# A graph layer's first stage in pairs of node columns, its node update in runs of consecutive nodes, its flag in the loop, its last groups in batches of their own

## The chip, the cores and the metric

The kernel runs on one core of one Trainium2 chip. The metric is the device time of one execution in microseconds (us), the median of several runs. A core has TensorE (PE, with its weight loads shown apart as PEld), VectorE (DVE), ScalarE (ACT), GpSimd (POOL) and SyncE (SP), each with an instruction queue of its own, and 16 DMA engines.

## What is computed

One layer of a graph network on 12,500 nodes of 64 features and 412,500 edges of 32 features, the edges sorted by receiver (`dst`):

```python
h = jnp.maximum(_layernorm(x, axis=-1), 0.0)
msg_in = jnp.concatenate([h[src], h[dst], edge_attr_32], axis=-1)
messages = act(msg_in @ W1 + b1) @ W2 + b2
att_logits = act(msg_in @ Wa1 + ba1) @ Wa2 + ba2
att = jax.nn.softmax(att_logits, axis=0)
aggregated = jax.ops.segment_sum(messages * att, dst, num_segments=12500)
upd_in = jnp.concatenate([h, aggregated], axis=-1)
return x + (act(upd_in @ Wu1 + bu1) @ Wu2 + bu2)
```

`act` is swish, and the softmax runs over all edges. Everything is float32.

## The kernel before

Nodes lie as `(p b)`: partition p holds NB = 98 consecutive nodes, and a "node column" b is one node of each of the 128 partitions. Edges lie in NG = 403 groups of K = 8 blocks of 128.

**First stage** (L168 to L243). Seven chunks of CB = 14 node columns are loaded (`xc`, L175), normalised on VectorE and ScalarE (L204 to L218), and transposed on TensorE, four columns to a PSUM tile `pt` (L224). VectorE copies that to `hT` (L225), whose row 64 is a one for the bias, set by GpSimd (L184). One matmul for each column (L228) multiplies it with the sender half of `w_node`; ScalarE copies the result to `ts` (L230), and SyncE writes it to the table `ts_d` (L231); `hT` goes to `hT_d` chunk by chunk (L232). In the third chunk `windows` (L186) makes each edge's place in its group's window (`dloc`) and a number for the flag. Then the same matmuls with the receiver half give `tr` and the table `tr_d` (L233 to L243).

**Loop over groups** (`one_pass`, L513). `load` (L351), two groups ahead, gathers 8 blocks of sender rows out of `ts_d` with 8 indirect DMAs issued by GpSimd (L358) into one of 8 buffers `gs`, loads a window of `tr_d` and the edge features through SyncE, and multiplies them on TensorE (L385) with a selection matrix made on VectorE (L381). `begin` (L390) adds both and starts tanh on ScalarE; swish is taken as x(1 + tanh x) on halved weights. `end` (L393) makes the message (L399), then the attention logits (L402 to L407). Four groups make a batch; `top` (L411) takes a batch's maximum through a transposition on TensorE, and `weigh` (L425) its weights. `sum_up` (L488), about five groups behind, does for one group after another `out_of` (L455, ScalarE), `put` (L465, VectorE, adds to `sums` and notes the maximum used), `project` (L460, TensorE) and `by_node` (L440: eight weight matrices on VectorE, then the matmuls of L452). `batch`, `starts` and `size` say which groups share a batch: fours, then groups 400 and 401, then group 402. From the third last group on, L534 to L539 do the sums left over. `pin` keeps these instructions in the order of the program. PSUM tiles named `mt` share one buffer. From group 16 on, `node_bias` (L252) and `node_rest` (L267) prepare for every four node columns the parts of the update that do not depend on the edges.

**Node update** (L553 to L596). Thirteen steps of eight node columns (the last of two). `fac` (L576, ScalarE) is the exponential that brings a node's sum to the last maximum. Two products on VectorE (L581) of `sums`, one over the total, and `fac` give `uT`, four columns on each half of the partitions; `bu` is added (L584), tanh on ScalarE (L586), a product (L587), a matmul for each pair of columns (L591), `x` added (L593), result out (L596). `sums` is stored by node, so node column b is every 98th element.

**Flag** (L599 to L608). The largest entry of `far` decides whether the general method must run afterwards. Three tiles named `res` stand between, so that their buffers' writes are waited for; `wrong` is loaded by all engines (L246) and a branch follows (L248).

Of the kernel before, what the change touches and what calls it, by code (L numbers as in the profile page):

```python
# [43 lines left out]
ALU = mybir.AluOpType  # L45
# [29 lines left out]
def gnn_kernel(ctx: ExitStack, tc: tile.TileContext, n_edges, x, src, dst, dst_row, first, edge,  # L75
# [14 lines left out]
    hT_d = dram.tile([D, NB, P], F32, name="hT_d")  # L90
    bu_d = dram.tile([U, NB, P], F32, name="bu_d")
    xb_d = dram.tile([NP, D], F32, name="xb_d")
# [5 lines left out]
    w_node = const.tile([D + 1, 2 * C + U], F32, name="w_node")  # L98
    nc.vector.memset(w_node[D:D + 1, C:2 * C], 0.0)
    nc.sync.dma_start(w_node[:D, 0:U], Wa1[0:D, :])  # L100
    nc.sync.dma_start(w_node[:D, U:C], W1[0:D, :])
    nc.sync.dma_start(w_node[D:D + 1, 0:U], ba1[None, :])
    nc.sync.dma_start(w_node[D:D + 1, U:C], b1[None, :])
    nc.scalar.dma_start(w_node[:D, C:C + U], Wa1[D:2 * D, :])
    nc.scalar.dma_start(w_node[:D, C + U:2 * C], W1[D:2 * D, :])
    nc.scalar.dma_start(w_node[:D, 2 * C:], Wu1[0:D, :])
    nc.scalar.dma_start(w_node[D:D + 1, 2 * C:], bu1[None, :])

    nc.vector.tensor_scalar(w_node[:, 0:2 * C], w_node[:, 0:2 * C], 0.5, None, op0=ALU.mult)
# [16 lines left out]

    wa2 = across(Wa2, U, "wa2")
# [40 lines left out]
    with tc.tile_pool(name="node1", bufs=1) as node1, \  # L168
# [14 lines left out]
        hT = node1.tile([D + 1, NB, P], F32, name="hT")  # L183
        nc.gpsimd.memset(hT[D:D + 1], 1.0)  # L184
# [14 lines left out]

        for c in range(0, NB, CB):  # L200
            if c == min(2 * CB, NB - CB):
                windows()
# [17 lines left out]
            for b in range(0, CB, 4):  # L220
                n = min(4, CB - b)
                pt = node_ps.tile([D, 4, P], F32, name="pt")
                for i in range(n):
                    nc.tensor.transpose(pt[:, i, :], h[:, b + i, :], ident)  # L224
                nc.vector.tensor_copy(hT[:D, c + b:c + b + n, :], pt[:, :n, :])  # L225
                pn = node_ps.tile([P, 4, C], F32, name="pn")
                for i in range(n):
                    nc.tensor.matmul(pn[:, i, :], hT[:, c + b + i, :], w_node[:, 0:C],  # L228
                                     start=True, stop=True)
                nc.scalar.copy(ts[:, b:b + n, :], pn[:, :n, :])  # L230
            nc.sync.dma_start(ts_d.rearrange("(p b) f -> p b f", b=NB)[:, c:c + CB, :], ts)  # L231
            nc.scalar.dma_start(hT_d[:, c:c + CB, :], hT[:D, c:c + CB, :])  # L232
        for c in range(0, NB, CB):  # L233
            tr = node.tile([P, CB, C], F32, name="tr")
            for b in range(0, CB, 4):
                n = min(4, CB - b)
                pn = node_ps.tile([P, 4, C], F32, name="pn")
                for i in range(n):
                    tc.keep_in_program_order(
                        nc.tensor.matmul(pn[:, i, :], hT[:, c + b + i, :], w_node[:, C:2 * C],  # L240
                                         start=True, stop=True))
                nc.vector.tensor_copy(tr[:, b:b + n, :], pn[:, :n, :])  # L242
            nc.scalar.dma_start(tr_d[:NP, :].rearrange("(p b) f -> p b f", b=NB)[:, c:c + CB, :], tr)  # L243
# [8 lines left out]
def node_bias(tc, b, v, work, ps):  # L252

    nc = tc.nc
    NB, w_node = v["NB"], v["w_node"]
# [3 lines left out]
    nc.sync.dma_start(hb[:D, :n, :], v["hT_d"][:, b:b + n, :])  # L259
    pb = ps.tile([P, 4, P], F32, name="mt")  # L260
    nc.tensor.matmul(pb[:U, :n, :], w_node[:, 2 * C:], hb[:, :n, :], start=True, stop=True)
    bu = work.tile([U, 4, P], F32, name="bu")
    nc.scalar.copy(bu[:, :n, :], pb[:U, :n, :])
    nc.sync.dma_start(v["bu_d"][:, b:b + n, :], bu[:, :n, :])
# [13 lines left out]
def one_pass(tc, n_edges, v):  # L278
# [5 lines left out]
    ts_d, tr_d, bu_d, edge, dst_row = (v[k] for k in ("ts_d", "tr_d", "bu_d", "edge", "dst_row"))  # L284
# [4 lines left out]
    starts = list(range(0, NG - 1, B)) + [NG - 1]  # L289
# [5 lines left out]
    with ExitStack() as ctx:  # L295
# [27 lines left out]
        with tc.tile_pool(name="work2", bufs=2) as work2, \  # L323
# [69 lines left out]
            def end(g):  # L393

                s = batch[g]
                if g == starts[s]:
                    lgs[s] = small.tile([P, B * K], F32, name="lg")
                gs, th = gss.pop(g), pes.pop(g)
                pin(nc.vector.scalar_tensor_tensor(acts[g % ACTS][:, :, 0:U], th[:, :, U:C], 1.0,  # L399
                                                   gs[:, :, U:C], op0=ALU.add, op1=ALU.mult))  # L400
# [7 lines left out]
                if g == starts[s] + size[s] - 1:  # L408
                    mts[s] = top(s)

# [102 lines left out]
            for g in range(NG):  # L513
                more = None
                if done <= g - B - 1 and g < NG - 1 or g == NG - 2 and done < starts[batch[g]]:
                    more, done = sum_up(done), done + 1
                begin(g)
                if more:
                    next(more)
# [14 lines left out]
                if g >= NG - 3:  # L534
                    upto = starts[batch[g]] - 1 if g == NG - 3 else g + 1
                    for i in list(range(done, upto)) + [None, None] * (g > NG - 3):
                        for _ in sum_up(i):
                            pass
                    done = max(done, upto)  # L539
# [4 lines left out]
                if g == min(40, NG):  # L544
                    pin(nc.vector.tensor_reduce(far[:, 1:2], dloc, AX.X, ALU.min, negate=True))
                if g >= 16 and g // 4 - 4 < -(-NB // 4):
                    if g % 4 == 2:
                        node_bias(tc, (g // 4 - 4) * 4, v, work2, one_ps)
# [4 lines left out]
        with tc.tile_pool(name="upd1", bufs=1) as upd1, \  # L553
# [4 lines left out]
            sv = sums[:, :NP].rearrange("f (p b) -> f b p", b=NB)  # L558
# [3 lines left out]
            all_ps = upd_ps.tile([P, P], F32, name="worst_ps", bufs=1)  # L562
# [4 lines left out]
            assert NB % 2 == 0  # L567
            for c in range(0, NB, 2 * H):
                n = min(H, (NB - c) // 2)
                bu = work.tile([P, H, P], F32, name="bu_in")  # L570
                for h in range(2):
                    nc.sync.dma_start(bu[h * U:(h + 1) * U, :n, :], bu_d[:, c + h * n:c + (h + 1) * n, :])
                xb = work.tile([P, 2 * H, D], F32, name="xb")
                nc.sync.dma_start(xb[:, :2 * n, :], xb_v[:, c:c + 2 * n, :])
                fac = work.tile([U, 2 * H, P], F32, name="fac", bufs=2)
                nc.scalar.activation(fac[:, :2 * n, :], sv[U:, c:c + 2 * n, :], AF.Exp, bias=last[U:],  # L576
                                     scale=-1.0)
                uT = work.tile([P, H, P], F32, name="uT")
                for h in range(2):
                    cols = slice(h * n, (h + 1) * n)  # L580
                    nc.vector.scalar_tensor_tensor(  # L581
                        uT[h * U:(h + 1) * U, :n, :], sv[:U, c + h * n:c + (h + 1) * n, :], inv[:U],
                        fac[:, cols, :], op0=ALU.mult, op1=ALU.mult)
                nc.vector.tensor_tensor(uT[:, :n, :], uT[:, :n, :], bu[:, :n, :], ALU.add)  # L584
                th = work.tile([P, H, P], F32, name="th", bufs=2)
                nc.scalar.activation(th[:, :n, :], uT[:, :n, :], AF.Tanh, scale=0.5)  # L586
                nc.vector.scalar_tensor_tensor(uT[:, :n, :], th[:, :n, :], 1.0, uT[:, :n, :],  # L587
                                               op0=ALU.add, op1=ALU.mult)
                po = upd_ps.tile([P, H, 2, D], F32, name="po")
                for i in range(n):  # L590
                    nc.tensor.matmul(po[:, i, :, :], uT[:, i, :], wu2h, start=True, stop=True)  # L591
# [7 lines left out]
            worst = upd1.tile([P, 1], F32, name="worst")  # L599
            nc.vector.tensor_reduce(worst, far, AX.X, ALU.max)  # L600
# [226 lines left out]
```

## Time and profile before

| what | us |
|---|---|
| median of 3 runs | 4208.31 (4206.68 to 4211.77) |
| the profiled execution | 4211.1, its span 4209.4 |
| GpSimd busy | 3059.3 (73%) |
| VectorE busy | 2907.0 (69%) |
| TensorE matmuls busy | 2308.4 (55%) |
| ScalarE busy | 595.9 (14%) |
| DMA | mean 93 GB/s |

A line of groups reads: line, engine, operation, output and inputs, count, then busy time in us and the mean of one in ns, then the idle time of the engine before them and what ended most of it. A line of the timeline or of the chain of waits begins with start and duration in us. A line of waits reads: engine, tile and line, what it waited for, total us, times, longest. A matmul in float32 leaves two records.

### The profile page before, as it was taken

The page shows a single profiled execution, that of the slowest core. Times are in us where ns is not written, and L with a number is a line of the kernel's source. Part 1 is how long each engine was busy: PE and PEld are TensorE (multiplying, and loading weights), DVE is VectorE, ACT ScalarE, POOL GpSimd, SP SyncE. Part 2 cuts the span into 40 slices and gives each one's busy share as a digit, 9 for nine tenths or more (in the row PEclk, how much of TensorE's full clock was granted, in tenths as well). Part 3 has the DMA queues.
Part 4 walks back from the last instruction along what each step waited for, and adds up shares of the span by engine and source line. Part 5 has one row for each costly group of instructions (what it writes and reads, how often), then busy time and mean ns, then how long its engine had stood idle before and what let it go on. Part 6 is the DMA issues. An engine that isn't in the chain of part 4 may idle for free.

```text
span 4209.4 us, 44290 instructions
## 1 busy us (share of the span) xinstructions
PE 2308.4 (55%) x11224; PEld 1739.7 (41%) x11224; DVE 2907.0 (69%) x7735; ACT 595.9 (14%) x1212; POOL 3059.3 (73%) x3237
## 2 busy tenths in 40 slices
PE   7645554554555555555555555555554555555554
PEld 6434433443334443444434434444443444344443
DVE  6666766766767766766667667667676666676667
ACT  2211111111111111111111111111111111111113
POOL 2777777777777777777777777777777777777771
PEclk8666676666666656656566556655566565556665
DMA  5533333333333333233333332333333333323323
GB/s 192 147 91 101 95 103 102 94 103 101 95 94 91 81 90 89 80 90 83 86 89 82 88 89 80 89 87 82 90 82 88 89 80 90 89 80 89 84 71 101
DMA packets 227026, 392.13 MB, mean 93 GB/s; under 512 B 98889, under 2 KB 151178, under 8 KB 213706
## 3 DMA queue, kind: packets, MB, share of 16 engines
q0 software_dynamic: 103168, 211.49, 18.8%
q1 hardware_dynamic: 120580, 167.79, 15.0%
q10 hardware_dynamic: 3014, 9.92, 0.8%
q8 instruction: 93, 1.52, 0.2%
q14 instruction: 171, 1.40, 0.1%
HBM read 363.16 MB, written 25.72 MB: 92 GB/s over the span
## 4 chain that ended last, share of the span: by engine, by line
POOL 43%; issue 22%; DMA 18%; DVE 12%; PE 5%; DVEq 0%; ACT 0%; POOLq 0%; SPq 0%; ACTq 0%
POOL gs L358 43%; DMA gs<-ts_d,src_sb 18%; PE pe L385 2%; DVE gs L390 2%; DVE eo L381 2%; DVE wt L446 1%; PE sp L452 1%; DVE pe L402 1%; DVE lg L407 1%; DVE pe L404 1%; PE pn L228 1%; DVE sums L477 1%; DVE uT L581 0%; DVE acts L399 0%; PE mt L463 0%
## 5 line engine op out<-in xcount | busy, mean ns | idle before, releaser
L358 POOL DMA_INDIRECT gs<-ts_d,src_sb x3224 | 3047.3, 945 | 1058.0 <-issue 884.7
L385 PE MATMUL pe<-wins,eo 128*128 128x256 f32 x3224 | 1410.9, 614 | 1137.8 <-issue 1096.1
L385 PEld LDWEIGHTS pe<-wins,eo 128*128 128x128 f32 x3224 | 960.3, 312 | 1417.0 <-issue 1144.0
L390 DVE TENSOR_TENSOR gs<-pe,gs 128x1024 f32<-128x1024 f32 x403 | 491.9, 1221 | 1112.1 <-DMA gs<-ts_d,src_sb 1103.6
L391 ACT ACTIVATE pe<-gs 128x1024 f32<-128x1024 f32 x403 | 413.3, 1026 | 2782.2 <-DVE gs L390 2347.1
L446 DVE TENSOR_SCALAR wt<-iota_w,dloc,p 128x40 f32<-128x40 f32 x3224 | 724.6, 316 | 0.1
L452 PE MATMUL sp<-wt,acts 128*65 128x40 f32 x6448 | 599.7, 264 | 2.6 <-DVE wt L446 2.6
L452 PEld LDWEIGHTS sp<-wt,acts 128*65 128x65 f32 x6448 | 548.4, 176 | 29.1 <-DVE wt L446 3.1
L422 PE MATMUL mt<-ident,mx 128*128 128x128 f32 x102 | 48.5, 475 | 524.8 <-DVE sums L476 513.5
L404 DVE TENSOR_TENSOR pe<-pe,wa 128x512 f32<-128x512 f32 x403 | 281.6, 699 | 12.8
L402 DVE SCALAR_TENSOR_TENSOR pe<-pe,gs 128x512 f32<-128x512 f32 x403 | 280.6, 696 | 11.3
L399 DVE SCALAR_TENSOR_TENSOR acts<-pe,gs 128x512 f32<-128x512 f32 x403 | 271.8, 674 | 19.0 <-ACT pe L391 18.4
L407 DVE TENSOR_REDUCE lg<-pe 128x8 f32<-128x512 f32 x403 | 277.0, 687 | 10.4
L381 DVE TENSOR_SCALAR eo<-db,bj 64x256 f32<-64x256 int32 x806 | 269.9, 372 | 7.6
L463 PEld LDWEIGHTS mt<-ss,w2u 65*64 65x64 f32 x806 | 101.7, 179 | 384.8 <-issue 375.5
L422 PEld LDWEIGHTS mt<-ident,mx 128*128 128x128 f32 x102 | 18.6, 182 | 538.2 <-DVE sums L476 526.0
L463 PE MATMUL mt<-ss,w2u 65*64 65x40 f32 x806 | 153.1, 284 | 148.8 <-DVE gm L429 146.5
L433 ACT ACTIVATE scale<-fall 128x1 f32<-128x1 f32 x102 | 20.7, 203 | 511.2 <-DVE fall L432 511.2
L477 DVE COPY sums<-nmax 64x40 f32 x403 | 77.4, 192 | 8.7
L458 ACT COPY ss<-sp 65x40 f32<-65x40 f32 x403 | 73.4, 182 | 24.4 <-PE sp L452 24.1
L476 DVE TENSOR_TENSOR sums<-sums,mt 64x40 f32 x301 | 53.7, 178 | 5.4 <-PE mt L463 4.2
L240 PE MATMUL pn<-w_node,hT 65*128 65x128 f32 x196 | 41.7, 410 | 1.0 <-DVE tr L242 0.8
(96 smaller groups left out, 699.1 us busy)
## 6 DMA issues: line engine op xcount, KB each, us to landing
gs<-ts_d,src_sb POOLq DMA_INDIRECT x3224
eo<-in_edge_dram SPq DMA_DIRECT2D x100, 512.0 KB
db<-in_dst_row_dram SPq DMA_DIRECT2D x200, 256.0 KB
wins<-tr_d SPq DMA_DIRECT2D x806, 32.0 KB
ts_d<-ts SPq DMA_DIRECT2D x7, 896.0 KB
tr_d<-tr ACTq DMA_DIRECT2D x7, 896.0 KB
xc<-in_x_dram SPq DMA_DIRECT2D x7, 448.0 KB
hT_d<-hT ACTq DMA_DIRECT2D x7, 448.0 KB
```

The costliest lines, as they stand in the source:

```text
L358: nc.gpsimd.indirect_dma_start(out=gs[:, j, :], out_offset=None, in_=ts_d[:, :], in_offset=bass.IndirectOffsetOnAxis(ap=src_sb[:, t + j:t ...
L381: pin(nc.vector.tensor_scalar(eo[:WR, e], db[:, e], bj[:, g, h:h + 1], None, op0=ALU.is_equal))
L385: pin(nc.tensor.matmul(pe[:, 2 * q:2 * q + 2, :], eo[:, q * P:(q + 1) * P], win[:, q // 2, :, :], start=True, stop=True))
L390: pin(nc.vector.tensor_tensor(gss[g], pes[g], gss[g], ALU.add))
L391: pin(nc.scalar.activation(pes[g], gss[g], AF.Tanh))
L399: pin(nc.vector.scalar_tensor_tensor(acts[g % ACTS][:, :, 0:U], th[:, :, U:C], 1.0, gs[:, :, U:C], op0=ALU.add, op1=ALU.mult))
L402: pin(nc.vector.scalar_tensor_tensor(att, th[:, :, 0:U], 1.0, gs[:, :, 0:U], op0=ALU.add, op1=ALU.mult))
L404: pin(nc.vector.tensor_tensor(att, att, wa2[:, None, :].to_broadcast([P, K, U]), ALU.mult))
L407: pin(nc.vector.tensor_reduce(lgs[s][:, k:k + K], att, AX.X, ALU.add))
L446: pin(nc.vector.tensor_scalar(wt[:, j, :], iota_w[:, j // H, :], dloc[:, g * K + j:g * K + j + 1], p[:, k + j:k + j + 1], op0=ALU.is_equal ...
L452: pin(nc.tensor.matmul(sp, acts[g % ACTS][:, j, :], wt[:, j, :], start=j == 0, stop=j == K - 1))
L463: pin(nc.tensor.matmul(pp, w2u, sps.pop(g), start=True, stop=True))
```

## The change

- *First stage.* Two neighbouring node columns are transposed together (128 rows). `hT` holds pairs, without the row of ones. `w_pair` holds the weights twice on the diagonal, zeros elsewhere, so one matmul 256 wide serves two columns. ScalarE copies `hT`; PSUM tiles `pn` have three buffers. The sender table gets no bias; VectorE adds both biases in the copy of `tr`. `windows` comes behind the seven chunks, and `hT_d` is written in one transfer behind them. `node_bias` loads its part of `hT_d` in two transfers.
- *Node update.* The eight columns of a step are taken as runs of eight (or four) consecutive nodes: `fac`, `uT`, `bu` are stored node by node, column innermost. `node_bias` stores its result so in `bq_d`, and the matmul reads its weights `uv[:, :, i]` four elements apart.
- *Flag.* It is worked out at groups 44 and 45; at the end three memsets of one column take the `res` buffers.
- *Last groups.* Groups 400, 401 and 402 are batches of their own, and the sums left over are dealt to groups 399 to 402. In group 402 the message comes behind the logits, and `out_of` ahead of `begin`.

```diff
-    hT_d = dram.tile([D, NB, P], F32, name="hT_d")
+    hT_d = dram.tile([2 * D, NB // 2, P], F32, name="hT_d")
+    bq_d = dram.tile([U, NP], F32, name="bq_d")
...
+    w_pair = const.tile([P, 2, 2, C], F32, name="w_pair")
+    nc.vector.memset(w_pair, 0.0)
+    for r in range(2):
+        for h, eng in ((0, nc.sync), (1, nc.scalar)):
+            rows = slice(h * D, (h + 1) * D)
+            eng.dma_start(w_pair[rows, r, h, 0:U], Wa1[r * D:(r + 1) * D, :])
+            eng.dma_start(w_pair[rows, r, h, U:C], W1[r * D:(r + 1) * D, :])
...
-        nc.gpsimd.memset(hT[D:D + 1], 1.0)
...
+        nc.vector.tensor_scalar(w_pair, w_pair, 0.5, None, op0=ALU.mult)
         for c in range(0, NB, CB):
-            if c == min(2 * CB, NB - CB):
-                windows()
...
+            for b in range(0, CB, 8):
+                n = min(8, CB - b)
+                q = (c + b) // 2
+                pt = node_ps.tile([P, 4, P], F32, name="pt")
+                for i in range(n // 2):
+                    nc.tensor.transpose(pt[:, i, :], h[:, b + 2 * i:b + 2 * i + 2, :], ident)
+                nc.scalar.copy(hT[:, q:q + n // 2, :], pt[:, :n // 2, :])
+                for i in range(0, n, 4):
+                    m = min(4, n - i)
+                    pn = node_ps.tile([P, 4, C], F32, name="pn", bufs=3)
+                    for k in range(0, m, 2):
+                        nc.tensor.matmul(pn[:, k:k + 2, :], hT[:, q + (i + k) // 2, :], w_pair[:, 0],
+                                         start=True, stop=True)
+                    nc.scalar.copy(ts[:, b + i:b + i + m, :], pn[:, :m, :])
             nc.sync.dma_start(ts_d.rearrange("(p b) f -> p b f", b=NB)[:, c:c + CB, :], ts)
-            nc.scalar.dma_start(hT_d[:, c:c + CB, :], hT[:D, c:c + CB, :])
+        nc.scalar.dma_start(hT_d, hT)
+        nc.vector.tensor_scalar(bias, bias, 0.5, None, op0=ALU.mult)
+        windows()
...
-                nc.vector.tensor_copy(tr[:, b:b + n, :], pn[:, :n, :])
+                nc.vector.tensor_tensor(tr[:, b:b + n, :], pn[:, :n, :],
+                                        bias[:, None, :].to_broadcast([P, n, C]), ALU.add)
...
-    nc.sync.dma_start(hb[:D, :n, :], v["hT_d"][:, b:b + n, :])
+    for r in range(2):
+        nc.sync.dma_start(hb[:D, r:n:2, :], v["hT_d"][r * D:(r + 1) * D, b // 2:(b + n) // 2, :])
...
+    if quads and n == 4:
+        nc.scalar.copy(bu.rearrange("u b p -> u (b p)").rearrange("u (p b) -> u b p", b=4), pb[:U])
...
-    starts = list(range(0, NG - 1, B)) + [NG - 1]
+    starts = list(range(0, NG - 3, B)) + [NG - 3, NG - 2, NG - 1]
...
+                if g < NG - 1:
+                    message()
...
                     mts[s] = top(s)
+                if g == NG - 1:
+                    message()
...
-                if done <= g - B - 1 and g < NG - 1 or g == NG - 2 and done < starts[batch[g]]:
+                if done <= g - B - 1 or g >= NG - 3 and done < g:
                     more, done = sum_up(done), done + 1
+                if more and g == NG - 1:
+                    next(more)
                 begin(g)
...
-                if g >= NG - 3:
-                    upto = starts[batch[g]] - 1 if g == NG - 3 else g + 1
-                    for i in list(range(done, upto)) + [None, None] * (g > NG - 3):
+                if g >= NG - 4:
+                    upto = g + (-3, -1, 0, 1)[g - NG + 4]
+                    for i in list(range(done, upto)) + [None, None] * (g == NG - 1):
                         for _ in sum_up(i):
                             pass
+                        if i == done and g < NG - 1:
+                            weigh_upto(batch[g])
...
+                if g == min(44, NG):
+
+                    worst = small.tile([P, 1], F32, name="worst", bufs=1)
+                    pin(nc.vector.tensor_reduce(worst, far, AX.X, ALU.max))
+                    worst_ps = one_ps.tile([P, 4, P], F32, name="mt")[:, 0, :]
+                    pin(nc.tensor.transpose(worst_ps, worst.to_broadcast([P, P]), ident))
+                if g == min(45, NG):
+                    pin(nc.vector.tensor_reduce(worst, worst_ps, AX.X, ALU.max))
+                    pin(nc.vector.tensor_scalar(wrong, worst, 0.0, None, op0=ALU.is_gt))
...
-            sv = sums[:, :NP].rearrange("f (p b) -> f b p", b=NB)
+            sv = sums[:, :NP].rearrange("f (p b) -> f p b", b=NB)
...
+                    nc.sync.dma_start(bu[h * U:(h + 1) * U], bq_d[:, (c + h * n) * P:(c + (h + 1) * n) * P])
...
+                fac = work.tile([U, P * 2 * H], F32, name="fac", bufs=2)[:, :P * 2 * n].rearrange(
+                    "u (p b) -> u p b", b=2 * n)
+                nc.scalar.activation(fac, sv[U:, :, c:c + 2 * n], AF.Exp, bias=last[U:], scale=-1.0)
+                uT = work.tile([P, P * H], F32, name="uT")[:, :P * n]
+                uv = uT.rearrange("u (p b) -> u p b", b=n)
                 for h in range(2):
                     nc.vector.scalar_tensor_tensor(
+                        uv[h * U:(h + 1) * U], sv[:U, :, c + h * n:c + (h + 1) * n], inv[:U],
+                        fac[:, :, h * n:(h + 1) * n], op0=ALU.mult, op1=ALU.mult)
...
-                    nc.tensor.matmul(po[:, i, :, :], uT[:, i, :], wu2h, start=True, stop=True)
+                    nc.tensor.matmul(po[:, i, :, :], uv[:, :, i], wu2h, start=True, stop=True)
...
-            nc.vector.tensor_tensor(wrong, two[0][:, 0, 0:1], two[2][:, 0, 0:1], ALU.max)
+            for _ in range(3):
+                pin(nc.vector.memset(work.tile([P, 2 * H, D], F32, name="res")[:, 0, 0:1], 0.0))
```

## The prediction

> **What bounds the kernel now.** I read the page first, then the timeline of both ends, then the groups with shapes kept apart. On the page one group stands out, and GpSimd's waits hold one long entry:
>
> ```profile
> span 4209.4 us, 44290 instructions
> L358 POOL DMA_INDIRECT gs<-ts_d,src_sb x3224 | 3047.3, 945 | 1058.0 <-issue 884.7
> ...
> POOL gs L358 <- DMA ts_d<-ts: 75.7, 1, 75.7
> ```
>
> The 3,224 gathers run on GpSimd one after the other. The first starts at 88.73 and waits for the table `ts_d`; the last, in the timeline:
>
> ```profile
> 88.73 1.10 POOL gs L358
> 4117.31 0.94 POOL L358 DMA_INDIRECT gs<-ts_d,src_sb  x1 [0.30 <-issue]
> ```
>
> 88.73 to 4118.25 is 4029.5 us, 1.250 each: 0.945 busy and 0.30 issue, and no wait after the first is longer than 0.3. GpSimd is saturated there; no other engine's work in the loop reaches the path. So the time is **head 88.7 + gathers 4029.5 + tail 91.2**, and the tail is 23.3 to the last `put` (4141.5), 56.0 to the last result (4197.5), 11.9 to the end. The span has 1.7 us around it (execution 4211.1), and the median of the runs is 2.8 below that execution.
>
> **Head.** The start (timeline, then chain of waits):
>
> ```profile
> 2.46 10.54 POOL L184 MEMSET hT<- 1x12544 f32 x1
> 4.10 9.05 DVE L109 TENSOR_SCALAR w_node<-w_node 65x256 f32<-65x256 f32 x1 [2.62 <-DMA w_node<-in_b_dram]
> 37.47 3.75 PE L228 MATMUL pn<-w_node,hT 65*128 65x128 f32 x16
> 55.35 2.02 PE L228 MATMUL pn<-w_node,hT 65*128 65x128 f32 x16 [0.43 <-DVE hT L225]
> ...
> 82.27 5.56 DMA ts_d<-ts
> 87.90 0.83 issue
> ```
>
> *Start.* L109 took 9.05 us and ended as the memset of `hT` ended; L116, half as wide, took 0.22. The change has no memset, and `w_pair` (128x512) is estimated at 0.5. The first node columns (DMA issued at 2.93; some 1.5 MB moved by 12 us at the rates of the stretches) should be there near 7, so the first reduction starts at 7 instead of 13.1: -6 (bounds 0 and -7). From it to the first transposition 10.3 us are kept: 17.3.
>
> *Pace.* Per chunk of 14 columns TensorE did 14 transpositions (8 in 1.92, 6 in 1.49) and 14 matmuls of 128 columns (3.75 + 2.90): 10.1 slow, 5.4 in the fast stretch (16 in 2.02). The pairs halve the transpositions (1.7 slow, 0.95 fast). Their 7 matmuls have the shape of L385, 128x256: 8 records in 3.56 to 3.75, or 1.97 fast, so 7 cost 6.4 or 3.45. The zero blocks are streamed as well, so the matmuls gain nothing. Sum 8.0 slow, 4.4 fast. VectorE loses the four copies of `hT` (3x0.68 + 0.41), 7.3 to 4.85 per chunk, and `windows` (6.4 us, 28.6 to 36.6) leaves its way. ScalarE gains `hT` copies of 0.58 + 0.48 and comes to 4.35. When TensorE is fast VectorE sets about 5.3 with the crossings; when slow TensorE sets 8.0.
>
> *Which clock.* The Trainium skill ("TensorE: Matmul & The Clock Gate", Part 1) has the array at full rate after some 3.4 us of sustained work. Here the rows speak against it: from 83.9 to 124.5 TensorE was busy without a gap (windows: 10.00 of 10) at 8 records per 1.71 us, half rate, granted 0.50; it was fast only from 48 to 65, and briefly near 80. By the rule seven chunks take 37 us, by slow rows 56. I take four slow and three fast, as before had it: 47.9, against 58.5 now. TensorE ends at 65.2.
>
> *Table out.* From the end of the matmuls to the first gather was 7.0. The transfer of `hT`, now 3.2 MB in one piece and issued by ScalarE about when the last 0.9 MB of `ts` goes out, shares the DMA engines. At some 310 GB/s (199 at a busy share of 0.64, windows 4170 to 4180) sharing evenly adds 2.9; bounds 0 and 10; I take 2.5. First gather at 65.2 + 7.0 + 2.5 = 74.7: **-14.0** (bounds -27 and +7).
>
> `windows` and the bias scaling now stand before the `tr` adds on VectorE, which has finished its chunks while TensorE still does its last; the add from PSUM costs L404's 0.70 against the copy's 0.69. The 49 `tr` matmuls take 44 slow, as now (42). Group 0 was finished 59 us after the first gather, and GpSimd first needs its buffer after 64 gathers, 80 us: 20 us of cover, then 1 us per us. Cost nothing.
>
> **Loop.** Nothing here, as GpSimd's queue holds gathers only. The flag (two small reductions, a transposition, a compare) and one more batch (about 1.2 us of VectorE) fall on a VectorE busy 68% between 1000 and 4000. `node_bias` issues one DMA more, 25 in all at 0.45 us, on SyncE's queue ahead of the windows of `tr_d`; SyncE waits 2034 us for L385 there. Its copy may rise from 0.58 to 1.2, ahead of the next tanh on ScalarE (13% busy). The flag holds the PSUM tile `mt` for one group, so a projection, and the sums behind it on TensorE, wait once. The cover is 8 gather buffers; without it each would cost its microseconds.
>
> **Last groups.**
>
> ```profile
> 4111.07 2.45 DMA gs<-ts_d,src_sb
> ...
> 4129.99 1.24 DVE gs L390
> 4141.33 0.19 DVE sums L477
> ```
>
> Landing is 2.45 after the start (first line, of an earlier gather), so the last gather is there at 4119.8, but group 402 begins at 4129.99: sums 399 to 401 stand ahead of it on VectorE, 400 and 401 waiting for a common maximum. In the new order, from group 400's start at 4099.94: own work 7.2, two sums (2.15 each), one weighing 0.65: 4112.3. Group 401: 6.7, one sum, one weighing: 4122. So 402 starts about 7.8 earlier. From there to the last `put` was 11.5. Sum 401 (2.15, half under the tanh) moves behind its start, and `out_of` ahead of its tanh makes ScalarE wait for sum 400's matmuls, together some +2.4; the message leaves the path, -0.7: 13.2. **-6.1** (bounds -3 and -8).
>
> **Node update.** The groups by shape:
>
> ```profile
> L581 DVE SCALAR_TENSOR_TENSOR uT<-sums,inv,fac 64x512 f32<-64x512 f32 x24 | 28.0, 1166 | 0.9 <-ACT fac L576 0.3
> L576 ACT ACTIVATE fac<-sums,nmax 64x1024 f32<-64x1024 f32 x12 | 26.8, 2239 | 12.0 <-DVE uT L581 10.8 <-DVE sums L477 1.1
> L587 DVE SCALAR_TENSOR_TENSOR uT<-th,uT 128x512 f32<-128x512 f32 x12 | 8.2, 681 | 0.1
> L591 PEld LDWEIGHTS po<-wu2h,uT 128*128 128x128 f32 x98 | 20.9, 314 | 33.2 <-issue 20.0 <-DVE uT L587 10.5 <-PE po L591 2.6
> ```
>
> VectorE is busy 9.84 of 10 here, 12.6 us per three steps. L581 reads `sums` every 98th element and takes 1166; L587, the same operation on 512 neighbouring elements, 681. The change reads runs of 4 (bounds 681 and 1166). The skill ("SBUF — State Buffer", Door 1) says that full rate needs two accesses per 16-byte line; a run of 4 gives each line it touches two or four. So 681: 2 x 0.485 x 12 = 11.6 saved. L576 should come to L391's 1026 plus a little; that lies under VectorE except the first, **-1.1**.
>
> The same rule speaks against the change elsewhere: `uv[:, :, i]` gives TensorE its weights at a step of 16 bytes, one access per line. Now 8 records take 1.78, under 2.08 of matmuls. With the roughly 1 ns per element that L581 and L576 show for such reading, 128 x 1 ns makes 8 loads 2.8, under VectorE's new 3.2. If the load doubles they take 3.6 and set the pace (saving 7). Transfers: 768 KB per step in 3.2 us is 240 GB/s of about 310. I allow 0.6 for both: **-11.0** (bounds -12 and a loss, below).
>
> **End.** Three memsets replace five operations behind the last output, and the engines other than VectorE can load the flag and branch before it. TensorE's branch is the longest:
>
> ```profile
> L248 PEldq COMPARE_BRANCH  x1: 4250/4250/4250, 4199.9 to 4199.9; - x1
> ```
>
> It could start up to 2.5 earlier; VectorE's own must still follow the memsets. **-1.5** (0 to -3).
>
> **Sum.** -14.0 - 6.1 - 1.1 - 11.0 - 1.5 = -33.7: 4211.1 to 4177.4 in the execution profiled, and against the median 4208.3 - 33.7 = **4174.6**.
>
> **Rivals.** (a) Runs of 4 don't pay, or the stepped weights double and more: the update saves 0 to 4 instead of 12, about 4184. For it: no row here shows a run of 4. Against: 681 against 1166 [...]. 0.17. (b) TensorE stays fast throughout the head: 11 earlier, 4163.6. For: 48 to 65. Against: 83.9 to 124.5. 0.15. (c) The head gains little, slow throughout and the whole `hT` transfer ahead of `ts`: 8 + 7.5 later, 4190. 0.12. (d) Slower than before: the stepped weights alone. At x us per load the update costs 98x when loads set its pace, against 53.7 now; the other parts save 22.7, so the break-even is 0.78 us a load, 3.5 times the present 0.22, and beyond 0.86 it is slower by over 0.2%. At 1.0 it gives about 4230. L581 and L576 show factors of 1.7 and 2.2 for stepped reading, against it. 0.03. (e) (a) and (c) both: about 4200, no difference. 0.03.
>
> **How the numbers follow.** My forecast has 0.50, (a) 0.17, (b) 0.15, (c) 0.12, (d) 0.03, (e) 0.03. The range 4160 to 4189 takes in (b) and (a) and most of (c). A measurement tells 0.2%, 8.4 us, from no change: faster 0.93, same 0.04, slower 0.03.
>
> **What would show it.** First gather near 75; 4029 us from it to the last; group 402's add near 2 us after its gather landed; the update's VectorE products near 0.68 and its steps near 3.3 with VectorE, not TensorE's loads, without gaps. I am wrong if the gather period moves from 1.250, if GpSimd waits near its 64th gather, or if the loads of L591 pass 0.4.

## The result, and the profile after

The changed kernel took **4179.99 us** (median of four runs, 4179.44 to 4181.06) against 4207.91 for the kernel before (four runs, one more than in the table above, 4206.68 to 4211.77). The ratio is 0.9932 with a 95% interval of [0.9915, 0.995]. The forecast was 4174.6.

The page of the changed kernel and GpSimd's timeline, first and last gather (start, duration, engine, line, idle time before and what ended it):

```profile
span 4177.7 us, 43813 instructions
...
L373 POOL DMA_INDIRECT gs<-ts_d,src_sb x3224 | 3047.1, 945 | 1055.2 <-issue 884.1
```

```profile
75.35 1.10 POOL L373 DMA_INDIRECT gs<-ts_d,src_sb  x1 [72.95 <-DMA tr_d<-tr]
...
4103.78 0.94 POOL L373 DMA_INDIRECT gs<-ts_d,src_sb  x1 [0.30 <-issue]
```

The gathers are the same 3,224 at the same pace: 75.35 to 4104.72 is 4029.4 us, as before. Everything gained lies ahead of the first and behind the last. (The releaser named in the first line is one of several awaited, and `tr_d` is not what this gather reads; e1 and e2 below bear on what it waits for.)

| stretch | before, us | after, us | change | forecast |
|---|---|---|---|---|
| to the first gather | 88.7 | 75.35 | -13.4 | -14.0 |
| gathers, first to last | 4029.5 | 4029.4 | -0.1 | 0 |
| last gather to last `put` | 23.3 | 17.3 | -6.0 | -6.1 |
| node update | 56.0 | 49.6 | -6.4 | -12.1 |
| last result to the end | 11.9 | 6.1 | -5.8 | -1.5 |
| span | 4209.4 | 4177.7 | -31.7 | -33.7 |

Three views show what the table hides. First the head: TensorE's seven series of matmuls, and the stretch from the last of them to the first gather (of the second, the columns after the length are PE, PEld, DVE, ACT and POOL busy, granted clock, DMA share, GB/s):

```profile
27.02 1.75 PE L228 MATMUL pt<-ident,h 128*128 128x128 f32 x7 [4.93 <-DVE h L220]
...
29.66 5.07 PE L234 MATMUL pn<-w_pair,hT 128*128 128x256 f32 x14 [0.89 <-ACT hT L229]
36.30 3.29 PE L234 MATMUL pn<-w_pair,hT 128*128 128x256 f32 x14 [0.81 <-ACT hT L229]
...
60.62 3.29 PE L234 MATMUL pn<-w_pair,hT 128*128 128x256 f32 x14 [0.35 <-ACT hT L229]
```

```profile
64.00:75.30 11.30, 8.54 (x40) 7.19 (x38) 4.81 (x8) 0.38 (x2) 0.00 (x0) 1.00 0.99 420
```

TensorE begins 3.6 us later than before (23.4). Only its first series is slow (5.07 against 3.29), and from 64 us on the DMA engines are full (0.99) at 420 GB/s.

The groups of the node update, shapes apart, in its 50 us, and behind them the last of the four as it was before the change:

```profile
L625 PEld LDWEIGHTS po<-wu2h,uT 128*128 128x128 f32 x98 | 23.8, 326 | 24.3 <-issue 16.8 <-DVE uT L622 7.3 <-PE po L625 0.2
L616 DVE SCALAR_TENSOR_TENSOR uT<-sums,inv,fac 64x512 f32<-64x512 f32 x24 | 17.8, 743 | 0.7
L612 ACT ACTIVATE fac<-sums,nmax 64x1024 f32<-64x1024 f32 x12 | 13.6, 1145 | 11.8 <-DVE uT L616 10.1 <-DVE sums L499 1.1
L627 DVE TENSOR_TENSOR res<-po,xb 128x512 f32<-128x512 f32 x12 | 8.3, 690 | 4.2 <-PE po L625 4.1
```

```profile
L593 DVE TENSOR_TENSOR res<-po,xb 128x512 f32<-128x512 f32 x12 | 8.2, 683 | 0.7 <-PE po L591 0.6
```

The product is down from 1166 to 743 ns, the factor from 2239 to 1145. The stepped weights load in 326 ns against 314 in the mean; e7 shows what that mean hides. New is the wait for `po`: VectorE, which before had 0.6 us of it, stands 4.1 us.

The end, by TensorE's branch and GpSimd's closing instructions. A line reads: line, queue, instruction, count, then the shortest, median and longest in ns, then the starts of the first and the last in us. The last line is of the kernel before:

```profile
L257 PEldq COMPARE_BRANCH  x1: 4232/4232/4232, 4171.2 to 4171.2; - x1
```

```profile
L849 POOLq DRAIN  x3: 40/107/3658, 4108.6 to 4177.4; - x3
```

```profile
L823 POOLq DRAIN  x3: 40/107/3658, 4204.9 to 4209.1; - x3
```

TensorE's branch takes 4.2 us as before, but begins 0.4 us ahead of the last result (before: 2.4 us behind it). GpSimd has its long DRAIN (3.66 us) at 4108.6, beside the last groups. Before, all three ran from 4204.9 to 4209.1 and closed the program.

### The profile page after: what moved, and what is told of

Same layout as the page of the kernel before. It is cut to its first block, busy times and chain, and to the rows that moved or that the text cites. A ratio compares the mean times of both kernels' runs of the same rounds, so it can differ in the third digit from the quotient of the medians.

```text
span 4177.7 us, 43813 instructions
## 1 busy us (share of the span) xinstructions
PE 2250.2 (54%) x10980; PEld 1686.0 (40%) x10980; DVE 2879.0 (69%) x7713; ACT 600.1 (14%) x1229; POOL 3048.7 (73%) x3236
## 4 chain that ended last, share of the span: by engine, by line
## 5 line engine op out<-in xcount | busy, mean ns | idle before, releaser
L474 PE MATMUL sp<-wt,acts 128*65 128x40 f32 x6448 | 586.0, 261 | 0.9 <-DVE wt L468 0.9
L474 PEld LDWEIGHTS sp<-wt,acts 128*65 128x65 f32 x6448 | 535.3, 173 | 27.0 <-DVE wt L468 1.0
L455 ACT ACTIVATE scale<-fall 128x1 f32<-128x1 f32 x103 | 20.9, 203 | 514.2 <-DVE fall L454 514.2
L275 ACT COPY bu<-mt 64x512 f32<-64x512 f32 x24 | 25.8, 1076 | 150.1 <-PE mt L272 144.4
```

The source lines that it names most:

```text
L474: pin(nc.tensor.matmul(sp, acts[g % ACTS][:, j, :], wt[:, j, :], start=j == 0, stop=j == K - 1))
```

## The experiments

The experiments used three chips. On two of them (every run except c0, e10 and e9) a group of the loop takes 13.0 us instead of 10.0, in the kernel before as well (5528 to 5556 us). The engines stand there for up to 20 us at a time for events that the trace doesn't name. What goes on outside the loop is not touched by it: in e3, e4, e5 and e7, which leave the head as it is or change only numbers in it, the first gather starts at 75.1 to 75.2, and the update takes 49.3 to 50.0 in e1, e2, e4, e5 and e6, which leave it as it is. So those runs are read by stage, and totals only where the loop takes 10 us.

### e1: constants issued by GpSimd

```diff
-    nc.scalar.dma_start(w_bu[:D, :], Wu1[0:D, :])
+    nc.gpsimd.dma_start(w_bu[:D, :], Wu1[0:D, :])
...
-    nc.scalar.dma_start(tr_d[NP:, :], zero[:WR, :])
+    nc.gpsimd.dma_start(tr_d[NP:, :], zero[:WR, :])
```

> The constants' loads from w_bu to tr_d<-zero are issued by GpSimd instead of ScalarE. Theory: in the changed kernel the first transposition (27.0 us, before 23.4) waits for ScalarE, whose queue issues these loads ahead of its first Square; with four issues left there it is ready at 17 to 19, the seven chunks then take 5.3 us each, and the first gather starts some 8 us earlier (67 instead of 75.35): time about 4172. Rival 1: the x loads set the start (the second half of x lands at 20 to 24 whatever ScalarE does): first transposition at 23 to 25, first gather 2 to 3 us earlier, about 4177. Rival 2: TensorE started earlier gets a lower clock or the transfers of ts and hT are the bound from there: first gather unchanged, about 4180.

ScalarE's timeline in the changed kernel, issues of transfers (ACTq) and work:

```profile
12.60 0.70 ACTq L136 DMA_DIRECT2D w2b<-in_W_dram  x1
16.27 0.25 ACTq L137 DMA_DIRECT2D w2b<-in_b_dram  x1
16.56 0.47 ACTq L139 DMA_DIRECT2D wu1a<-in_Wu_dram  x1
17.08 0.66 ACTq L141 DMA_DIRECT2D wu<-in_Wu_dram  x1
20.30 0.55 ACTq L161 DMA_DIRECT2D tr_d<-zero  x1
20.88 1.28 ACT L213 ACT_TABLE_LOAD   x1 [20.88 <-DMA wu1a<-in_Wu_dram]
```

and in e1:

```profile
3.63 0.62 ACTq L107 DMA_DIRECT2D w_pair<-in_W_dram  x1
4.28 1.28 ACT L213 ACT_TABLE_LOAD   x1 [4.28 <-issue]
6.84 0.95 ACT L213 ACTIVATE sq<-xm 128x896 f32<-128x896 f32 x1 [1.27 <-DVE xm L211]
```

```profile
64.57 1.03 POOL L373 DMA_INDIRECT gs<-ts_d,src_sb  x1 [47.27 <-DMA ts_d<-ts]
```

In the changed kernel the queue itself stands between issues, 3.0 us from 13.3 to 16.3 and 2.6 us from 17.7 to 20.3, and ScalarE's first work comes behind its last issue. What the queue waited for in these two gaps no trace here names. With four issues left ScalarE starts at 4.28, the first transposition comes at 15.60 (27.02) and the first gather at 64.57: 10.8 earlier, somewhat more than the theory's 8. Both rivals fall.

### e2: hT_d written last

```diff
-        nc.scalar.dma_start(hT_d, hT)
...
+            tc.keep_in_program_order(nc.scalar.dma_start(tr_d[:NP, :]..., tr))
+        tc.keep_in_program_order(nc.scalar.dma_start(hT_d, hT))
```

> The write of hT_d (3.1 MB) is issued after the last write of tr_d instead of ahead of the last copies of ts. Theory: in the changed kernel 63.9 to 75.35 is bound by the transfers (DMA share 0.91 to 0.99), and those of hT_d take their part beside the ts_d writes that the first gather waits for; without them this stretch is some 3 to 5 us shorter, the first gather at 71 to 72, time about 4176. Rival: the stretch is the fixed latency of the last ts_d write and the gather's own start, and hT_d only fills idle engines: first gather within 1 us of 75.35, time 4180. A cost of the late hT_d could show in the loop (first loads of hb wait); neither theory expects over 1 us of it.

The same stretch in e2, last matmul of `ts` to first gather, and that gather:

```profile
64.00:68.50 4.50, 4.50 (x23) 3.96 (x22) 3.35 (x6) 0.00 (x0) 0.00 (x0) 1.00 0.62 255
```

```profile
68.54 1.10 POOL L373 DMA_INDIRECT gs<-ts_d,src_sb  x1 [66.14 <-issue]
```

From the end of TensorE's last matmul of `ts` (63.46 here, 63.91 in the changed kernel) the first gather takes 5.1 us instead of 11.4, at a DMA share of 0.62 instead of 0.99. That is 6.4 us, more than the theory's 3 to 5; the first gather comes 6.8 earlier because the chunks ended 0.45 earlier as well. So most of the stretch was a wait for the last pieces of `ts_d`, which shared full engines with 3.2 MB of `hT`. The first write of `tr_d`, issued at 67.6 in the changed kernel, joined them; its part was not tried apart.

### e5, e6, e11: what made the pace

e5 fills the zero blocks of `w_pair` with the other half's weights (so `ts` and `tr` are other numbers):

```diff
+        for h in range(2):
+            rows = slice(h * D, (h + 1) * D)
+            nc.vector.tensor_copy(w_pair[rows, :, 1 - h, :], w_pair[rows, :, h, :])
```

> The two zero blocks of the weights for the pairs of columns hold the other half's weights instead of zeros, so ts and tr are other numbers than the reference's; instructions, shapes and order are unchanged. Theory that zeros are what lets TensorE run at the full granted clock (1.00 up to 75 us, before 0.53 from 65): the granted clock in 27 to 92 us falls to 0.5 to 0.8 in part of it, and the first gather comes 3 to 15 us later (4183 to 4195). Rival: the contents don't matter, only how TensorE is loaded: first gather within 1 us of 75.35, 4179 to 4181.

e6 issues each `ts` matmul as two:

```diff
-                        nc.tensor.matmul(pn[:, k:k + 2, :], hT[:, q + (i + k) // 2, :], w_pair[:, 0],
-                                         start=True, stop=True)
+                        for r in range(2):
+                            nc.tensor.matmul(pn[:, k + r, :], hT[:, q + (i + k) // 2, :], w_pair[:, 0, r],
+                                             start=True, stop=True)
```

> Each matmul of ts over a pair of columns (256 wide) is issued as two of 128 with the same stationary operand; the same result. Theory: the pace of 5.3 us per chunk is set by ScalarE's and VectorE's copies and the granted clock, not by the number of matmuls: first gather within 1.5 us of 75.35, 4179 to 4182. Rival: the number of TensorE's instructions sets the pace and the clock; with it back at 14 per chunk more the chunks take up to 8.0 us as in the kernel before: first gather up to 15 us later, up to 4195.

e11 gives the copies of `hT` back to VectorE:

```diff
-                nc.scalar.copy(hT[:, q:q + n // 2, :], pt[:, :n // 2, :])
+                nc.vector.tensor_copy(hT[:, q:q + n // 2, :], pt[:, :n // 2, :])
```

> The 14 copies of hT in the first stage are done by VectorE, as before the change, instead of ScalarE; the pairs of columns stay. The halved matmuls of the narrow form left the pace at 5.3 us a chunk, so something else of this part made it. Theory: the move of the copies off VectorE, which is 90 to 99% busy from 30 to 50 us: with 14 copies of 0.55 to 0.65 us (8 to 9 us) back on it, the first gather is 6 to 9 us later, 81 to 84. Rival: VectorE has the copies' time to spare behind 50 us (4.9 of 10 busy) and the pairs themselves (half as many transpositions, copies twice as full) made the pace: first gather within 2 us of 75.2.

The first gather of e5, e6 and e11:

```profile
75.19 1.10 POOL L376 DMA_INDIRECT gs<-ts_d,src_sb  x1 [72.78 <-DMA tr_d<-tr]
```

```profile
74.70 1.10 POOL L374 DMA_INDIRECT gs<-ts_d,src_sb  x1 [72.30 <-DMA tr_d<-tr]
```

```profile
77.25 1.10 POOL L373 DMA_INDIRECT gs<-ts_d,src_sb  x1 [74.85 <-DMA tr_d<-tr]
```

The zeros make no difference (75.19), nor does the number of `ts` matmuls (74.70): in both runs the series of matmuls behind the first stay fast (3.29 and 3.39 us). The copies on ScalarE are worth 2.0 to 2.1, not the theory's 6 to 9: the 14 copies are 8.6 us of VectorE, but it had room behind 50 us. The theory falls. Of the rival, that VectorE had the time to spare is borne out; that the pairs made the pace is not shown by this.

The seven chunks took 21.6 us less than before (58.5, now 36.9). About 2 come from the engine of the copy. By the records most of it is TensorE's rate: before, four chunks had some 10.1 us of TensorE's work and three 5.4, a difference of 19 us over the four, and now all series but the first are fast. What kept TensorE fast stays open. Half as many transpositions of 128 rows, the third buffer of `pn`, and `windows` behind the chunks were not tried apart. A hint is a pause of TensorE: in e11 one of 2.63 us, and in e1 one of 2.80, are followed by a slow series (4.95 and 4.98), while the pauses in the changed kernel's chunks, at most 1.27, are not. It doesn't explain the kernel before, where TensorE worked from 35.5 to 42.5 without a pause and stayed slow.

### e3, e9: the wait for po

e3 writes the update as three stages, so that a whole step lies between a run's matmuls and the addition of its result (`xb` has five buffers for it):

```diff
...
+            for c in list(range(0, NB, 2 * H)) + [None, None]:
+                new = products(c) if c is not None else None
+                if one:
+                    nxt = apply(*one)
+                if new:
+                    new = tanh(*new)
+                if two:
+                    result(*two)
+                two, one = (nxt if one else None), new
```

> The node update is issued by hand in three stages: the products of a run of nodes, then the (tanh+1)*u of the run before, then the addition of po of the run before that. Theory: the 4.1 us that VectorE waits for po come from an order in which the shorter products no longer cover TensorE's 2.1 to 2.2 us; with a whole step between, the wait is gone, a step takes VectorE's own work (3.2 to 3.4 us instead of 3.87), and 4122 to 4171.6 shrinks by 5 to 6 us: about 4174. Rival 1: TensorE at half clock or the stepped weights pace the stage: the wait moves to another place and the time stays at 4179 to 4181. Rival 2: the transfers of res and bu pace it: waits on DMA in place of those on TensorE, 4178 to 4181.

The waits of e3 in its update (total, times, longest):

```profile
DVE uT L616 <- ACT fac L612: 9.7, 11, 1.9
DVE res L636 <- PE po L631: 1.6, 1, 1.6
```

The wait for `po` is gone but for the last step, and yet the update took 55.8 instead of 49.6. The order that I had written put the factor of the next run (1.15 us) behind the tanh of this one on ScalarE, and VectorE waited for it in 11 steps. Neither the theory nor a rival had this. e9 issues the factor first (shown beside e3; it also has the edits of e1 and e2):

```diff
                 if one:
                     nxt = apply(*one)
+                if after is not None:
+                    fac = factors(after)
                 if new:
                     new = tanh(*new)
```

> The same head, and the update in three stages by hand with the factor of the next run issued on ScalarE ahead of the tanh of this one. Theory (the update by hand was slower by 6.0 us only because its order made VectorE wait 9.7 us for the factor, not for TensorE): no wait for the factor, 3.4 to 3.5 us a step, node update 45.5 to 47 us instead of 49.6. Rival 1: a wait for po or the transfers takes the place: 49 to 51. Rival 2: ScalarE's factor and tanh together still hold VectorE up: 52 to 56.

```profile
L620 DVE SCALAR_TENSOR_TENSOR uT<-sums,inv,fac 64x512 f32<-64x512 f32 x24 | 17.8, 740 | 0.3
...
L640 DVE TENSOR_TENSOR res<-po,xb 128x512 f32<-128x512 f32 x12 | 8.2, 684 | 1.5 <-PE po L635 1.5
```

No wait for `po` but the last (1.5) and one of 1.3 for `bu_in`, steps of 3.35 us, update 45.9: inside the theory's 45.5 to 47. All its groups of eight loads took 1.94 us, as at half clock. So TensorE's half clock does not pace this stage; only the order made VectorE wait for it.

### e7: weights read in a row

```diff
-                    nc.tensor.matmul(po[:, i, :, :], uv[:, :, i], wu2h, start=True, stop=True)
+                    nc.tensor.matmul(po[:, i, :, :], uT[:, i * P:(i + 1) * P], wu2h, start=True, stop=True)
```

> TensorE takes the stationary operand of the node update's matmuls from 128 consecutive words instead of words 16 bytes apart, so that rows of the output are permuted within a run of nodes and are not the reference's. Theory: the stepped read costs next to nothing (326 against 314 ns a load): the update shrinks by less than 1.5 us, 4178.5 to 4180. Rival: the stepped read is what paces TensorE's 2.1 to 2.2 us and with it the 4.1 us that VectorE waits: the update shrinks by 4 to 6 us, 4174 to 4176.

The update took 46.0, 3.6 less: between the two numbers. Two stretches with the full clock granted, of the changed kernel and then of e7, each with eight loads and eight matmuls:

```profile
4134.10:4136.10 2.00, 1.99 (x8) 1.94 (x8) 1.48 (x2) 1.15 (x1) 0.00 (x0) 1.00 0.84 284
```

```profile
5420.30:5421.30 1.00, 0.95 (x8) 0.97 (x8) 0.97 (x2) 0.22 (x1) 0.00 (x0) 1.00 0.82 309
```

At half clock the step costs little: eight loads take 1.94 us against 1.78, and a matmul record is 437 ns against 421, some 0.13 us a step and 1.7 in all if each nanosecond were on the path. At the full clock it doubles the loads. Read in a row, eight loads take 0.97 us and their matmuls 1.13, in e7 three times and in the kernel before once (at 4169.72). Stepped, they take 1.94 at a granted 1.00 as at 0.50, in the changed kernel and in every run with its weights. So the stepped update gets nothing from a rise of the clock: three groups of matmuls at 1.13 us instead of 2.2 are 3.2 us, which with the step's own cost is enough for the 3.6. In windows of 3.5 us e7 shows three rises of the granted clock, the changed kernel and every run with its update two; whether reading in a row earns the third or it came by chance stays open. That VectorE's wait for `po` fell (4.1 to 1.7 over the full steps) agrees with e9: it hangs on TensorE's speed only as long as nothing else is put between.

### e4: the flag at the end

```diff
-                if g == min(44, NG):
...
+            worst = upd1.tile([P, 1], F32, name="worst")
+            nc.vector.tensor_reduce(worst, far, AX.X, ALU.max)
...
+            nc.vector.tensor_tensor(wrong, two[0][:, 0, 0:1], two[2][:, 0, 0:1], ALU.max)
```

> The flag is put back behind the outputs, as in the kernel before; all else is as changed. The prediction put this part at 1.5 us. Theory after the result: with the flag early, TensorE's branch and GpSimd's closing DRAIN run beside the last outputs, so the end is worth all of the 11.9 - 6.1 = 5.8 us: time about 4186, last result to end of span 11 to 12 us, the DRAIN of 3.66 us behind the last output again. Rival (the prediction's): +1.5 us, 4181.5, and the 5.8 came from elsewhere, so that the end stays at 7 to 8.

Last result, TensorE's branch and GpSimd's DRAIN in e4 (span 5458.1):

```profile
5446.07 0.29 DVE L618 TENSOR_TENSOR res<-po,xb 128x128 f32<-128x128 f32 x1 [0.64 <-PE po L616]
```

```profile
L257 PEldq COMPARE_BRANCH  x1: 4135/4135/4135, 5448.7 to 5448.7; - x1
```

```profile
L848 POOLq DRAIN  x3: 40/107/3658, 5453.6 to 5457.8; - x3
```

5446.4 to 5458.1 is 11.7, close to the 11.9 of the kernel before, with the branches 2.3 behind the last result and the DRAIN behind GpSimd's own. The early flag alone is worth 5.6, not 1.5.

### c0, e10, e9: the whole on a chip where a group takes 10 us

e10 is e1 and e2 together; e9 adds the update, and e8 is e10 with the update of e3.

> Three edits together: constants issued by GpSimd, hT_d written after tr_d, and the update in three stages by hand. Theory: -8 (start), -3 (hT_d), -5 (update): 4162 to 4167. Rival: earlier start and freed transfers lead to the same wait for the table, so that they don't add (-6 to -8 together with the update's -5 or 0): 4167 to 4173; if all three rivals hold, 4177 to 4181.

e8's first gather was at 57.43, 17.9 earlier, so the two head edits add; its update took 55.8 as in e3. Its total, on a chip where the loop takes 13 us, says nothing more.

> The changed kernel, unaltered, so that the next two have it beside them. Both theories: first gather at 75.1 to 75.4 us, node update 49.3 to 49.9, last result to the end 5.9 to 6.4, whatever the loop between them takes (10.0 us a group in the profiles of before and after, 13.0 in the runs so far).

> Constants issued by GpSimd and hT_d written after tr_d, the update as in the changed kernel. Theory (the two edits were worth 10.6 and 6.8 us alone, and don't meet): first gather at 57.4, and as GpSimd's gathers run without a gap from there where the loop takes 10.0 us a group, the time is 17 to 18 below the changed kernel's (about 4162 against 4180; where the loop takes 13 us, hidden in its scatter). Rival: the loop can't use it: the 128-wide stage for the window rows ends as late as before, the first groups wait for it, and the gathers stall once the buffers are full: first gather at 57.4, but the last gather less than 8 us earlier, time 4172 to 4180.

First and last gather in c0, e10 and e9:

```profile
75.03 1.10 POOL L373 DMA_INDIRECT gs<-ts_d,src_sb  x1 [72.63 <-DMA tr_d<-tr]
...
4104.69 0.94 POOL L373 DMA_INDIRECT gs<-ts_d,src_sb  x1 [0.30 <-issue]
```

```profile
57.66 1.03 POOL L373 DMA_INDIRECT gs<-ts_d,src_sb  x1 [40.19 <-DMA ts_d<-ts]
...
93.62 0.94 POOL L373 DMA_INDIRECT gs<-ts_d,src_sb  x1 [2.45 <-DMA gs<-ts_d,src_sb]
...
4088.12 0.94 POOL L373 DMA_INDIRECT gs<-ts_d,src_sb  x1 [0.30 <-issue]
```

```profile
57.81 1.03 POOL L373 DMA_INDIRECT gs<-ts_d,src_sb  x1 [40.58 <-DMA ts_d<-ts]
...
4093.02 0.94 POOL L373 DMA_INDIRECT gs<-ts_d,src_sb  x1 [0.30 <-issue]
```

| | median, us | ratio to before, 95% | update | last result to end |
|---|---|---|---|---|
| before | 4215.59 | | | |
| c0, as changed | 4183.97 | 0.9915 [0.99, 0.993] | 49.3 | 6.1 |
| e10 | 4169.53 | 0.9881 [0.9863, 0.9899] | 49.9 | 7.4 |
| e9 | 4164.31 | 0.9867 [0.9849, 0.9885] | 45.9 | 6.3 |

c0 repeats the result. In e10 the first gather is 17.4 earlier and the last 16.6: one wait of 2.45 for an earlier gather's transfer, while `tr_d` and `hT_d` go out, is the only long new one in GpSimd's gathers, and the loop keeps the rest. The rival (the last gather less than 8 earlier) falls. The medians are 14.4 apart, not the theory's 17 to 18; the profiled executions are 15.2 apart, with an end that is 1.3 longer (7.4). e9 has the lowest median here, 19.7 below the changed kernel's, but its interval overlaps that of e10. In its profiled execution the update's 4 us hardly show, because the gathers took 4035.2 from first to last start against 4030.5 in e10: behind the first 403, each 403 took 504.0 to 504.5 instead of 503.4 to 504.0, with no line that names a cause.

## Why the prediction was right, and where it was wrong

**Sum.** The steps gave -33.7 and the profiled executions differ by 31.7. That closeness is in part luck: the update fell 5.7 short of its forecast and the end went 4.3 beyond. The other 3.4 of the 5.4 between forecast and median are a choice of base: the profiled execution of before lay 2.8 above its median, that of after 0.6 below its own.

**Head: right by three errors that cancel.** Forecast 74.7, measured 75.35.
*Start*, 17.3 forecast, 27.02 measured (+9.7): the step took "the first transposition 10.3 us" behind the first reduction. The reduction did start early, at 4.31, but I had left ScalarE's queue out of the chain. Before, its 19 issues ended at 13.64, half a microsecond behind the slow L109; the change made them 23, ending at 20.85. e1 shows that it was this.
*Pace*, 47.9 forecast, 36.9 measured (-11.0): rival (b), the array "fast throughout", is what happened, but for the first series. The page's row of the granted clock is no help here: in the kernel before, 37 to 48 us was granted 1.00 and yet 16 matmuls took 3.75, as many as 2.02 later on. The rule of the Trainium skill that I set aside ("TensorE: Matmul & The Clock Gate", Part 1: full rate after some 3.4 us of sustained work) fits the changed head, where one series of 5.07 is followed by six of 3.29; the 37 us that I had worked out by it are the 36.9 measured. It doesn't fit the 41 gapless microseconds at half rate in the kernel before. I generalised from that stage; it had a granted clock of 0.50 for the most part, and the chunks of the changed kernel had 1.00 throughout. What decides between the two stays open.
*Table out*, 9.5 forecast, 11.4 measured (+1.9): the mechanism, "shares the DMA engines", is right, its size is not. Without `hT` the stretch is 5.1 (e2) where I had kept 7.0, and the transfer cost 6.4 where I had taken 2.5. The even sharing failed: 3.2 MB at the measured 420 GB/s are 7.6 us, and most of that was paid. My rate of 310 GB/s, worked out from a stretch with a share of 0.64, was too low, but that error alone would have made the forecast too long.

**Loop: right.** 4029.4. The flag and the extra batch cost nothing, as said.

**Last groups: right**, -6.0 for -6.1, by two smaller errors that cancel.

```profile
4109.32 1.22 DVE L405 TENSOR_TENSOR gs<-pe,gs 128x1024 f32<-128x1024 f32 x1 [0.21 <-issue]
```

Group 402 begins here, some 3 us behind its gather's landing where the forecast's sign was 2. Counted from the last gather's end that is 7.1 earlier than before, not 7.8 (the parts of the forecast's sum give 4112.1, not 4112.3); from there to the last `put` it is 12.7, not 13.2.

**Node update: wrong by 5.7.** Two terms. "So 681" was 743: 24 x 0.062 = 1.5. And the sum took VectorE to be without gaps, while it waits 4.1 for `po`. The prediction looked for a bound in the weights' load and in the transfers; it did not ask what the removed work had covered. One step, before and after:

```profile
4156.99 2.37 DVE L581 SCALAR_TENSOR_TENSOR uT<-sums,inv,fac 64x512 f32<-64x512 f32 x2
4157.02 2.08 PE L591 MATMUL po<-wu2h,uT 128*128 128x128 f32 x8 [1.39 <-DVE uT L587]
4159.29 0.67 DVE L593 TENSOR_TENSOR res<-po,xb 128x512 f32<-128x512 f32 x1
```

```profile
4145.54 1.52 DVE L616 SCALAR_TENSOR_TENSOR uT<-sums,inv,fac 64x512 f32<-64x512 f32 x2
4145.65 2.21 PE L625 MATMUL po<-wu2h,uT 128*128 128x128 f32 x8 [1.48 <-DVE uT L622]
4147.89 0.69 DVE L627 TENSOR_TENSOR res<-po,xb 128x512 f32<-128x512 f32 x1 [0.84 <-PE po L625]
```

Two products of 1.17 lay over TensorE's 2.1 to 2.2 us of matmuls; two of 0.74 do not, in an order that was fixed when the program was built. e9 shows it: with another order, 45.9 against the forecast's 43.9, and of the 2.0 left 1.5 are the product. The stepped loads cost less at half clock than the prediction's estimate (1.94 us for eight, estimated 2.8). At the full clock they doubled, a case that its sum did not have, and read in a row they leave 1.7 of the wait (e7).

**End: wrong by 4.3.** The step counted when the branch "could start up to 2.5 earlier" and let GpSimd's DRAIN stay. e4 shows 5.6 for the flag alone: the branch comes forward by 2.8 against the last result, and the rest is the DRAIN. In the kernel before it had to follow GpSimd's own branch, which waited for the flag (4199.9); now that branch comes at 4096.8.

**Rivals.** (d) falls by the 326 ns of a load. (a) falls in its first half, as runs of 4 took 743 ns and not 1166. Its second half, the stepped weights, holds in part: read in a row, the update was 3.6 shorter (e7). Its number, 4184, lies nearer to the 4180.0 measured than the forecast's 4174.6. (b) holds for the pace (-11.0), (c) for most of the transfer (6.4 of its 7.5). That the first gather still came near 75 is luck: the late start (+9.7) took back what the pace had won.

## What to carry to other kernels

When work is taken off the bounding engine, ask what that work was covering: the faster engine waits next for whatever ran under it, in the order that stands. Here putting a step between gave back some 4 of the 5.7 us that were missing. ScalarE's first instruction stood behind every transfer that it issued (20.9 us, with four issues left 4.3), so the head of a kernel is read from the queues of issues, not only from the chain of arithmetic. Where only the start of a saturated stream counts, keep large transfers that nobody waits for out of the stretch before it.

## What the runs showed that I had not expected

- An engine's closing work can be moved under the outputs: 5.6 us here, by letting the branch be decided early (TensorE's branch 4.1 to 4.25 us, GpSimd's DRAIN 3.66 us).
- The kernel before takes 4216 us on one chip and 5528 to 5556 on two others. In the changed kernel's variants this comes of the loop: 13.0 us a group instead of 10.0, with gathers of 945 ns as ever and waits that the trace doesn't name.
- Sixteen DMA engines at a share of 0.99 moved 420 GB/s.
- A step of 16 bytes in TensorE's weights costs eight loads 0.16 us at half clock (1.94 against 1.78) and doubles them at the full clock (1.94 against 0.97). A read 392 bytes apart costs VectorE 485 ns on top of 681, runs of four words 62.
